# A priority for the layer norms of a chain of four attention blocks

## The chip, the cores and the metric

The kernel runs on one core of one Trainium2 chip. The metric is device time in microseconds (us) of one execution; the profile is of one further execution of the same kernel. Engines are named as in the profile: PE (TensorE matmul), PEld (its weight loads), DVE (VectorE), ACT (ScalarE), POOL (GpSimd) and SP (SyncE, which issues DMAs).

## What is computed

For 64 examples, x is 128 rows of 128 numbers and the context has 77 rows of 128. Four blocks follow one another, and each contains layer norms:

```python
# block 0
norm_X   = ln(context, norm1);  norm_F = ln(x, norm2)
cross    = gelu(attention(norm_F, norm_X, norm_X) @ fc1.T + b) @ fc2.T + b
norm_c   = ln(cross, norm3)
x = norm_F + gamma2 * (cross + gamma1 * attention(norm_c, norm_c, norm_c))
# block 1
x = ln(x + linear_attention(elu(x), elu(context), context), gamma, beta)
# block 2
q = ln(x, sa_ln);                x = x + mha16(q, q)            # 16 heads of 8
x = x + mha16(ln(x, ca_q_ln), ln(context, ca_kv_ln))
x = x + mixture_of_8_experts_top2(ln(x, moe_ln))
# block 3
x1 = ln(x + mha16_causal(x, x), g1)
x2 = ln(x1 + mha16(x1, context), g2)
out = ln(x2 + relu(x2 @ W1 + b1) @ W2 + b2, g3)
```

A layer norm takes each row's mean and variance over 128 numbers, then (row - mean) / sqrt(variance + 1e-5), times a scale, plus a shift.

## The kernel before

**Tiling.** Four examples make a group (NB = 4), so there are 16 groups, and two groups make a set (SG = 2) for the experts. A tile of a group is 128 partitions by 4 x 128 numbers.

**Stages.** `front` is blocks 0 and 1 for a group, `middle` the two attentions of block 2 and the router, `dispatch` and `experts` the mixture for a set, and `second_half` adds the experts' answers and does block 3. Each is a Python generator that yields between steps. The main loop at the end of the program takes one step of each in turn: `firsts` (the middle of group t beside the front of group t+1), `sends` (dispatch), `seconds` (experts), and one or two lanes of `second_half`. So the code records its instructions with the steps of several groups interleaved.

**Order.** A scheduler then gives every engine one list of instructions. Each instruction gets a rank, a counter at the place where the code records it. Where several instructions of an engine are ready at once, the scheduler takes the one of lowest rank. It also finds the tiles their places in memory: a tile name has a fixed number of buffers, and its user waits for one to be free. On the chip every engine works through its own list, with semaphores between the engines.

**The norm.** `normalize` (L269) does the part of a layer norm before scale and shift. For its four examples it has 13 instructions on DVE and one on POOL: four statistics (L274, tile `st`), four means and variances (L276, `mv`), the addition of epsilon (L278, `ve`), the power -0.5 on POOL (L280, `rs`), and four (x - mean) * rs (L283, tile `xh`, or `xm` for the expert norm). `st`, `mv`, `ve` and `rs` have 4 buffers each, `xh` two, `xm` three. It is called 10 times per group, 160 times in all: for C (the context, L470), X (L501), ca (L526), xa (L576, whose scaled result is x1), x1 (L583, for the self-attention of block 2), x2 (L586, cross-attention), x3 (L591, experts) and three times in `second_half` (L830 and L835 after the two attentions, L842 at the end).

**What follows a norm.** Mostly `transposed` (L292): four transposes on PE (L296) into a PSUM tile `bank` (three buffers, used by nearly all PE work), then a scaled copy by ACT (`affine_t`, L303). `affine` (L288) scales and shifts the untransposed result on DVE (L289, L290; in two places L290 is on POOL).

**Other work named below.** In `mha`: the projections (L340, L344), KX (L349 on DVE, L353 on ACT), `vpad` (L364), the bias added to the residual on POOL (L371), then per example the scores (L387, into `banks`), maximum (L396), difference (L398), exp (L399), transposes (L409) and their copies pT (L410), the weighted sum (L417), the copy oT (L425), transposes (L428), division (L431, L432), and at the end the output projection (L456) and the residual add (L460). In `front`: kp (L487, L491), ca (L524), xa (L571). In `middle`: the router and its gates (L595 to L622), their transposes (L627), gT (L629), the product with the experts' bias (L632) and x3b (L634). In `dispatch`: L671 to L733 on DVE, and the indirect DMAs of POOL to the experts' rows (L739). In `experts`: L782, L787, GELU he (L792), L794, the copy ye (L800). In `second_half`: indirect DMAs that fetch answers (L817), their addition to x4 (L821), the feed-forward (L645, L654, L840).

Of the kernel before, what the change touches and what calls it, by code (L numbers as in the profile page):

```python
# [69 lines left out]
def tile_xattn_chain(  # L70
# [197 lines left out]

    def normalize(src, p=P, pool=work, tag="xh", bufs=None):  # L269

        st = small.tile([P, NB, 6], F32, tag="st", name="st")
        mv = small.tile([P, NB, 2], F32, tag="mv", name="mv")
        for b in range(NB):
            V.bn_stats(st[:p, b, :], src[:, b, :])  # L274
        for b in range(NB):
            V.bn_aggr(mv[:p, b, :], st[:p, b, :])  # L276
        ve = small.tile([P, NB], F32, tag="ve", name="ve")
        V.tensor_scalar(ve[:p], mv[:p, :, 1], EPS, None, ALU.add)  # L278
        rs = small.tile([P, NB], F32, tag="rs", name="rs")
        G.tensor_tensor(rs[:p], ve[:p], mhalf[:p], ALU.pow)  # L280
        xh = pool.tile([P, NB, P], F32, tag=tag, name=tag, bufs=bufs)
        for b in range(NB):
            V.tensor_scalar(  # L283
                xh[:p, b, :], src[:, b, :], mv[:p, b, 0:1], rs[:p, b : b + 1], ALU.subtract, ALU.mult
            )
        return xh[:p]
# [180 lines left out]
    def front(st):  # L467
        X, C = st["X"], st["C"]
        Cx = C[:, :, 0:P]
        ch = normalize(Cx, SK)  # L470
        cps = transposed(ch, SK)
        nXT = work.tile([P, NB * SK], F32, tag="nXT", name="nXT", bufs=1)
# [26 lines left out]


        xh = normalize(X)  # L501
        nF = work.tile([P, NB, P], F32, tag="nF", name="nF", bufs=1)
        affine(nF, xh, "n2_w", "n2_b", G)
# [20 lines left out]
        V.tensor_tensor(ca, ps.rearrange("q (b d) -> q b d", b=NB), bc(row["fc2_b"], 1, NB), ALU.add)  # L524
        yield
        xh = normalize(ca)  # L526
        nxT = affine_t(xh, "n3_w", "n3_b")
        nx = work.tile([P, NB, P], F32, tag="nx", name="nx", bufs=1)
# [458 lines left out]
```

## Time and profile before

| | |
|---|---|
| median of 3 runs | 3913.91 us (3906.8 to 3919.5) |
| profiled execution, its own time | 3934.11 us |
| its span, first to last instruction | 3932.3 us |
| mean granted PE clock | 0.832 |
| DVE statistics L274 | 640 instructions of about 0.277 us |
| DVE mean and variance L276 | 640 of about 0.152 us |
| DVE L278 | 160 of about 0.18 us |
| POOL L280 | 160 of 1.027 us |
| DVE L283 | 640 of about 0.34 us at the median |

In the profile, a group's line gives the line of the program, the engine and the operation, then what it writes and reads, the count, the busy time and the mean time of one. The list of waits says which instruction waited for which: total us, times, and the longest. A line of the timeline gives start, duration, engine, line, operation and shapes, and in brackets how long the engine was idle before it and what ended that. Successive short instructions of DVE overlap a little, so four statistics of 0.277 us span some 0.87 us. PE matmul ends are modelled. Names in the trace carry no numbers: x stands for x1, x2, x3 and others.

### The profile page before, as it was taken

Reading aid. Unit: us, or ns where it says so; the run is one execution under the profiler, and the core shown is the slowest. Engines: PE = TensorE matmul, PEld = TensorE weight load, DVE = VectorE, ACT = ScalarE, POOL = GpSimd, SP = SyncE. Lnnn points to the kernel's source line nnn. Section 1 sums busy time; section 2 is a strip of 40 time slices with the busy share of each in tenths; the row PEclk is TensorE's granted clock in tenths of the full one; section 3 lists DMA queues with packets and bytes.
Section 4 is the critical chain, followed back from the end, with each engine's and each line's share of the span. In section 5 each row is a group of like instructions: output and inputs, shape, how many; then the busy total and the mean of one; then the engine's idle time right before and its main releaser. Section 6 shows DMA issues by size and latency. Waiting matters only on the chain. (4 is left out here: it accounts for less than half of the span.)

```text
span 3932.3 us, 59072 instructions
## 1 busy us (share of the span) xinstructions
PE 3022.6 (77%) x22735; PEld 2063.3 (52%) x22797; DVE 2153.0 (55%) x5292; ACT 1977.9 (50%) x2994; POOL 519.4 (13%) x506
## 2 busy tenths in 40 slices
PE   3675677778778778787778877878878888878777
PEld 2454455545455555555455555656545555545544
DVE  5656454456465564555556645566445635445354
ACT  2443353545365554555454635656446556536344
POOL 1002101110211101101211012010210121020110
PEclk9776776878788787978788977989778989989988
DMA  5001111110111111111111011111111132222100
GB/s 178 2 10 35 45 37 55 48 43 30 47 37 43 46 37 33 43 38 52 39 32 53 28 55 39 41 37 36 37 46 40 43 104 65 63 83 64 62 8 6
DMA packets 168257, 180.81 MB, mean 46 GB/s; under 512 B 15708, under 2 KB 111784, under 8 KB 167848
## 3 DMA queue, kind: packets, MB, share of 16 engines
q1 hardware_dynamic: 157936, 157.03, 12.8%
q0 software_dynamic: 8192, 16.79, 1.4%
q8 instruction: 181, 2.97, 0.3%
q10 hardware_dynamic: 1848, 3.19, 0.2%
q14 instruction: 100, 0.82, 0.1%
HBM read 133.54 MB, written 43.42 MB: 45 GB/s over the span
## 5 line engine op out<-in xcount | busy, mean ns | idle before, releaser
L410 ACT COPY pT<-bank 77x512 f32<-77x512 f32 (+1 forms) x1024 | 565.8, 584 | 454.1 <-PE bank L409 410.5
L409 PE MATMUL bank<-ident,pr 128*128 128x128 f32 (+1 forms) x4096 | 661.5, 304 | 146.6 <-ACT pr L399 89.1
L396 DVE TENSOR_REDUCE m<-banks 128x8 f32<-128x1024 f32 (+1 forms) x512 | 514.6, 1005 | 432.3 <-PE banks L387 431.7
L409 PEld LDWEIGHTS bank<-ident,pr 128*128 128x128 f32 (+1 forms) x4096 | 506.7, 158 | 358.8 <-ACT pr L399 134.4
L398 DVE TENSOR_TENSOR pr<-banks,m 128x1024 f32<-128x1024 f32 (+1 forms) x512 | 513.7, 1003 | 26.7 <-PE bank L409 3.1
L399 ACT ACTIVATE pr<-pr 128x1024 f32<-128x1024 f32 (+1 forms) x512 | 451.5, 888 | 122.9 <-DVE pr L398 120.7
L387 PE MATMUL banks<-KX,QT 32*128 32x512 f32 (+1 forms) x2048 | 450.7, 659 | 51.7 <-DVE pr L398 39.6
L280 POOL TENSOR_TENSOR rs<-ve,mhalf 128x4 f32<-128x4 f32 (+1 forms) x160 | 164.4, 1027 | 2379.7 <-DVE ve L278 2379.3
L417 PE MATMUL po<-pT,vpad 77*32 77x128 f32 (+1 forms) x8192 | 435.3, 290 | 17.9 <-issue 8.2
L417 PEld LDWEIGHTS po<-pT,vpad 77*32 77x32 f32 (+1 forms) x8192 | 246.1, 112 | 145.8 <-issue 109.0
L794 PE MATMUL bank<-we,he 128*128 128x128 f32 x1472 | 246.1, 318 | 63.8 <-ACT he L792 60.7
L794 PEld LDWEIGHTS bank<-we,he 128*128 128x128 f32 x1472 | 209.9, 220 | 131.5 <-ACT he L792 103.7
L787 PEld LDWEIGHTS bank<-xT,we 128*128 128x128 f32 x1472 | 229.8, 227 | 60.7 <-ACT xT L769 32.6
L787 PE MATMUL bank<-xT,we 128*128 128x128 f32 x1472 | 241.9, 316 | 18.5 <-ACT xT L769 14.4
L296 PE MATMUL bank<-ident,xh 128*128 128x128 f32 (+1 forms) x448 | 97.0, 340 | 196.5 <-DVE xh L283 179.7
L792 ACT ACTIVATE he<-bank 128x512 f32<-128x512 f32 x184 | 109.9, 597 | 236.0 <-PE bank L787 227.8
L431 DVE RECIPROCAL rs<-bank 128x16 f32<-128x16 f32 x256 | 64.8, 253 | 290.3 <-PE bank L428 286.1
L387 PEld LDWEIGHTS banks<-KX,QT 32*128 32x128 f32 x2048 | 135.9, 213 | 144.2 <-issue 92.4
L739 POOL DMA_INDIRECT sent<-xm,rows_i x128 | 126.0, 984 | 525.7 <-DVE m L396 168.7
L296 PEld LDWEIGHTS bank<-ident,xh 128*128 128x128 f32 (+1 forms) x448 | 64.9, 167 | 223.5 <-issue 161.3
L792 ACT ACT_TABLE_LOAD x124 | 159.1, 1283 | 37.5 <-PE bank L787 35.5
L303 ACT ACTIVATE tT<-bank,col_sb 128x512 f32<-128x512 f32 x80 | 62.3, 778 | 182.6 <-PE bank L296 172.8
(242 smaller groups left out, 4055.3 us busy)
## 6 DMA issues: line engine op xcount, KB each, us to landing
we<-in_moe_w_dram SPq DMA_DIRECT2D x368, 256.0 KB
sent<-zero SPq DMA_DIRECT2D x56, 192.0 KB
xe<-sent SPq DMA_DIRECT2D x56, 192.0 KB
answered<-ye SPq DMA_DIRECT2D x56, 192.0 KB
X<-in_x_dram SPq DMA_DIRECT2D x16, 256.0 KB
later_x<-x3b SPq DMA_DIRECT2D x16, 256.0 KB
x<-later_x SPq DMA_DIRECT2D x16, 256.0 KB
out_dram<-y SPq DMA_DIRECT2D x16, 256.0 KB
```

Of the source, the lines that this page charges most:

```text
L280: G.tensor_tensor(rs[:p], ve[:p], mhalf[:p], ALU.pow)
L296: T.transpose(ps[:, b * p : (b + 1) * p], src[:, b, :], ident[:p, :p])
L387: T.matmul(sc[:, g, : NJ * nk].rearrange("q (j k) -> q j k", j=NJ), lhsT=QT[part, b, :], rhs=KX[part, :, b, :nk], start=not is_causal, sto ...
L396: recent["max"] = V.tensor_reduce(m, scores, AX.X, ALU.max)
L398: V.tensor_tensor(pr, scores, bc(m, 3, nk), ALU.subtract)
L399: S.activation(pr, pr, AF.Exp, scale=DH**-0.5)
L409: T.transpose(pt[:nk, j * P : (j + 1) * P], pr[:, i, j, :], ident)
L410: S.copy(pT[:nk, i].rearrange("k j q -> k (j q)"), pt[:nk])
L417: T.matmul(po[32 * g : 32 * g + 32, half * P : half * P + P], lhsT=vp[:nk, b, 4 * half + g, 32 * k : 32 * k + 32], rhs=pT[:nk, g // 2, g % ...
L787: T.matmul(ps[:, c * P : (c + 1) * P], lhsT=we[:, 0, c, :], rhs=xT[:, a * P : (a + 1) * P], start=False, stop=c == NC - 1,)
L792: S.activation(he.rearrange("p c q -> p (c q)"), ps, AF.Gelu)
L794: T.matmul(eo[:, a * P : (a + 1) * P], lhsT=he[:, c, :], rhs=we[:, 1, c, :], start=c == 0, stop=c == NC - 1)
```

## The change

The body of `normalize` is moved into a function `normalized`, and `normalize` calls it inside a block of the scheduler's that lowers the rank by 400 for the instructions recorded in it. At the block's end the counter goes back to where it was. The instructions, tiles, buffers and engines are the same.

```diff
     def normalize(src, p=P, pool=work, tag="xh", bufs=None):
 
+        with tc.high_priority(offset=400):
+            return normalized(src, p, pool, tag, bufs)
+
+    def normalized(src, p, pool, tag, bufs):
         st = small.tile([P, NB, 6], F32, tag="st", name="st")
         mv = small.tile([P, NB, 2], F32, tag="mv", name="mv")
         for b in range(NB):
```

The lines below the change have numbers 4 higher in the kernel after.

## The prediction

> **What bounds the kernel now.** I read the page's first part, then the list of waits, then the groups by form, then stretches of the timeline on VectorE (DVE) and TensorE (PE).
>
> ```profile
> span 3932.3 us, 59072 instructions
> PE 3022.6 (77%) x22735; PEld 2063.3 (52%) x22797; DVE 2153.0 (55%) x5292; ACT 1977.9 (50%) x2994; POOL 519.4 (13%) x506
> ```
>
> ```profile
> PE bank L296 <- DVE xh L283: 179.7, 44, 11.2
> ...
> DVE xh L283 <- POOL rs L280: 146.8, 125, 7.0
> PEld bank L409 <- ACT pr L399: 134.4, 106, 8.6
> ```
>
> No engine is full. PE is busiest at 77%, so some 900 us of the span it stands idle, and the largest single cause is a layer norm: the transposes of L296 wait 179.7 us, 44 times, for the last instruction of a norm (xh, L283). With the waits for the expert norm's result (called xm, same line) it is 200.1 us, spread over 48 of the 160 norms. DVE in turn idles 146.8 us inside norms, waiting for the one operation they have on POOL (L280).
>
> What a norm costs alone, and what stands in its way, shows on DVE and PE here:
>
> ```profile
> 402.55 0.36 DVE L276 BATCH_NORM_AGGREGATE mv<-st 128x2 f32<-128x6 f32 x4
> 402.82 0.66 DVE L460 TENSOR_TENSOR x<-x,bank 128x512 f32<-128x512 f32 x1
> 403.39 0.17 DVE L278 TENSOR_SCALAR ve<-mv 128x4 f32<-128x4 f32 x1
> 403.51 0.29 DVE L274 BATCH_NORM_STATS2 st<-x 128x6 f32<-128x128 f32 x1
> 404.79 2.06 DVE L283 TENSOR_SCALAR xh<-xa,mv,rs 128x128 f32<-128x128 f32 x4 [0.98 <-POOL rs L280]
> 406.77 0.28 DVE L274 BATCH_NORM_STATS2 st<-x 128x6 f32<-128x128 f32 x1
> 406.97 0.67 DVE L289 TENSOR_TENSOR x<-xh,row_sb 128x512 f32<-128x512 f32 x1
> 407.56 0.28 DVE L274 BATCH_NORM_STATS2 st<-x 128x6 f32<-128x128 f32 x1
> 407.77 0.67 DVE L290 TENSOR_TENSOR x<-x,row_sb 128x512 f32<-128x512 f32 x1
> 408.36 0.28 DVE L274 BATCH_NORM_STATS2 st<-x 128x6 f32<-128x128 f32 x1
> 408.56 0.35 DVE L276 BATCH_NORM_AGGREGATE mv<-st 128x2 f32<-128x6 f32 x4
> 408.84 1.54 DVE L491 SCALAR_TENSOR_TENSOR kp<-kp,kr 77x512 f32<-77x512 f32 x1
> 410.31 0.15 DVE L278 TENSOR_SCALAR ve<-mv 128x4 f32<-128x4 f32 x1
> 411.66 1.11 DVE L283 TENSOR_SCALAR xh<-x,mv,rs 128x128 f32<-128x128 f32 x4 [1.20 <-POOL rs L280]
> ```
>
> ```profile
> 412.15 1.16 PE L296 MATMUL bank<-ident,xh 128*128 128x128 f32 x4 [10.81 <-DVE xh L283]
> ```
>
> The input of the second norm (x2) is complete at 403.5, and its last xh ends at 412.8. Between its four statistics stand L289, L290 and L491 of other streams, which nobody is waiting for, while PE stands idle for 10.81 us. A norm with nothing in between takes 1.35 us for statistics, mean and variance, 1.20 us until POOL has answered, and 1.11 us for the four xh: 3.7 us.
>
> **What the Trainium skill says.** "PSUM — Partial Sum Buffer", section "Engine vs sequencer instructions": the queues of ScalarE, VectorE and GpSimdE are strict FIFO, and matmuls start in program order. The trace agrees: the PE line above has nothing else between 401.3 and 412.2, so the scheduler's order decides, and an instruction that waits holds all behind it. [...]L280 works on four numbers per partition and takes 1.03 us, where DVE's L278, of the same shape, takes 0.17. "Perfetto Trace Analysis", section "Roofline": where matmul and HBM utilization are both low, the kernel is bound by latency. Here PE is at 77% busy, not low, but with 23% waits it agrees in part: what shortens a chain helps only if PE waits on it.
>
> **The change part by part.** Nothing is added or removed; durations stay. Each of the 160 norms issues 13 instructions on DVE and one on POOL, and no DMA. All get a rank 400 places earlier. The instructions executed around a norm lie mostly within some 150 places of its own place in the code's order, so 400 is more than every competitor has: a norm's instruction goes ahead of whatever is ready on its engine, and the true data waits remain.
>
> What it can't move: in the order as executed the first writers of each tile name stand in the order of the code, without exception (2,354 `bank` tiles, 160 `st` tiles). So the norms keep their order among themselves, and PE's users of `bank`, which are nearly all, keep theirs. The inputs C and X are loaded long before, but their norms start only after the norm before them, and this stays. I therefore expect no norm to run far ahead; only local reordering on DVE.
>
> *The gain.* For each of the 48 norms that PE waits for I added the DVE time of foreign instructions between the moment its input was written (and the norm before it had begun) and its last xh, leaving out what fits in the POOL answer. I took the smaller of that and the wait. By kind (norms, wait, removable): ca (L526) 9, 27.9, 20.1 us; x2 (L586) 10, 74.9, 22.2; x1 (L583) 3, 31.6, 0; x3 (L591) 9, 20.3, 2.1; 3s xs (L830) 8, 17.2, 5.9; 3c xs (L835) 9, 28.1, 5.5. Sum 55.8 us of 200.1. The rest is the norms' own 3.7 us, two in a row, or the residual add before. Waiting of L280 behind other work on POOL (indirect DMAs of L739 and L817 among it) adds at most 13 us; I take 0, since POOL is 13% busy and what delays it are waits, not rank. Bounds of the gain: 28 (half is late next for another reason) and 69.
>
> *The loss.* The foreign instructions go behind the norm. For every one that stood inside a norm I took the norm's DVE time still to come, where some engine's wait ended on exactly that instruction (no slack). On PE these are 23.7 us: scores waiting for L398 and others 6.3, x4 and O before L296 4.7, the router chain before L627 and L632 10.3, the start 2.4. On ACT they are 24.2 us (exp after L398 13.2, KX 4.4, gate 5.6 and less), of which half should reach PE: 12.1. Of all foreign time inside norms, 90.6 of 215.5 us belong to the C and X norms of the next group, whose results nobody waits for soon: there the change only costs. On POOL, L280 in front of an L371, L290 or indirect DMA costs these 1.03 us; their own waits are long, so I count 0, at most 10. On SP nothing is moved. Bounds of the loss: 12 (half of PE's part) and 58 (all of both, and POOL's 10).
>
> *Cost at nothing.* DVE will stall the 1.2 us for POOL in nearly all norms instead of 141 of 160: 19 x 1.2 = 23 us of DVE idle, covered since DVE has 45% idle; without cover it is in the bounds of the loss.
>
> *Sum.* 55.8 - 23.7 - 12.1 = 20.0 us. The profiled execution took 3934.1 us (3932.3 span and 1.8 around it), 20 us or 0.5% above the median of the runs, 3913.9. It would become 3914.1; from the median I predict 3894. Next late after a norm is ACT's scaled copy of the transposes (L303), as now.
>
> **The rivals.** *Absorbed:* PE's order is fixed, so PE resumes earlier and then waits as much longer for the next chain (exp L399 ends 89 us of PE waits, pT 42, he 61). For it: 700 us of PE's idle time belongs to other waits. Also here: the rank hardly bites, because few competitors are ready at once. Against: the foreign time inside norms is measured. Some 5 us remain: 3909.
>
> *Slower:* the C and X norms, and x1's, stand at the turn of each group together with the router chain (L597 to L629), on which PE waits at L627 and L632 for 23.8 and 16.0 us already:
>
> ```profile
> 2312.31 1.01 PE L627 MATMUL bank<-ident,gate 128*8 128x128 f32 x4 [6.40 <-DVE sums L678]
> ```
>
> X's statistics (1.35 us) and the rest of C's norm (0.8 + 1.1) would go ahead of that chain: 3.25 us in 16 turns are 52 us at most. With only half the gain, 28, and the whole of the no-slack delays, 23.7 + 24.2 = 48, it ends at +20: 3934. It decides from the point where the delay of these chains exceeds what PE saves at L296; on my numbers a doubled delay or a halved gain, with the ACT half arriving whole.
>
> *More than forecast:* the displaced work has slack after all (no loss): 3914 - 56 = 3858.
>
> **Chances.** Forecast (3870 to 3902) 0.40; more than forecast 0.08; absorbed 0.27; slower 0.25. The resolution is 0.3%, 12 us: faster is under 3902, slower over 3926. That gives faster 0.47, same 0.28, slower 0.25. The range goes from the full gain with little loss (3860) to the slower case (3938).
>
> **What would show it.** Right: L296's wait for xh falls from 200 to about 145 us, and foreign instructions between a norm's statistics and its xh disappear; x2's norm at the place shown takes 3.7 us instead of 9.3. The loss shows as more waiting at L627, L632, L387 and of ACT at L399; absorbed shows as PE idle still near 890 us with the share of L296 smaller. Wrong: if norms of C and X begin far earlier than the norm before them, or `bank` users change order on PE, my view of the fixed order is false, and the time can leave the range either way.

## The result, and the profile after

The kernel after took 3895.74 us (median of 12 runs, 3879.48 to 3905.65) against 3917.45 us for the kernel before beside it (12 runs, 3902.81 to 3924.71): a ratio of 0.9947, 95% interval 0.9931 to 0.9963. In a second session, with 11 and 40 runs, it was 0.9952 (0.9935 to 0.9969). So the change saves some 20 us; 3894 was predicted. The account behind that number does not hold, as the next sections show.

The page of the kernel after begins with these lines:

```profile
span 3893.9 us, 59149 instructions
PE 2985.6 (77%) x22797; PEld 2033.7 (52%) x22797; DVE 2153.9 (55%) x5292; ACT 1982.7 (51%) x2998; POOL 522.4 (13%) x506
```

The waits of the kernel after (instruction, what it waited for, total us, times, longest):

```profile
PEld bank L413 <- ACT pr L403: 151.4, 114, 11.3
PE bank L300 <- DVE xh L287: 131.6, 32, 11.1
...
DVE xh L287 <- POOL rs L284: 111.4, 114, 4.2
```

The wait at the transposes (L296 before, L300 now) fell from 179.7 to 131.6 us. DVE did not stall more on POOL, as predicted, but less: 146.8 us became 111.4.

The norm of x2 that the prediction showed, on DVE in the kernel after:

```profile
395.81 2.06 DVE L287 TENSOR_SCALAR xh<-xa,mv,rs 128x128 f32<-128x128 f32 x4 [0.84 <-POOL rs L284]
397.79 0.28 DVE L278 BATCH_NORM_STATS2 st<-x 128x6 f32<-128x128 f32 x1
398.00 0.36 DVE L280 BATCH_NORM_AGGREGATE mv<-st 128x2 f32<-128x6 f32 x4
398.27 0.65 DVE L293 TENSOR_TENSOR x<-xh,row_sb 128x512 f32<-128x512 f32 x1
398.85 0.16 DVE L282 TENSOR_SCALAR ve<-mv 128x4 f32<-128x4 f32 x1
398.92 0.68 DVE L495 SCALAR_TENSOR_TENSOR kp<-kp,kr 77x512 f32<-77x512 f32 x1
400.51 1.11 DVE L287 TENSOR_SCALAR xh<-x,mv,rs 128x128 f32<-128x128 f32 x4 [0.92 <-POOL rs L284]
```

and on PE:

```profile
401.00 1.15 PE L300 MATMUL bank<-ident,xh 128*128 128x128 f32 x4 [8.99 <-DVE xh L287]
```

The reordering is what was said: the kp of L495 (L491 before) now lies in the time in which POOL answers, and L294 comes after xh. The size is not. From the input's completion (394.19) to the last xh (401.62) the norm takes 7.4 us, against 9.3 before and 3.7 in the prediction, because the norm of xa, which has the priority too and is earlier in the code, still stands in it with its four xh (2.06 us) and its stall, and L293 besides. PE waits 8.99 us here, against 10.81. Over all 160 norms, the DVE time of foreign instructions between the first statistic and `ve` (other norms' instructions not counted) fell from 1.22 to 0.29 us per norm, and between the first and the last xh from 0.39 us to nothing.

**The same pair on one chip.** The first trace of the kernel before was its slowest run, so both kernels were traced again side by side (the experiments e5 and e11). The kernel before again:

```profile
span 3915.1 us, 59134 instructions
PE 3019.6 (77%) x22797; PEld 2060.7 (53%) x22797; DVE 2154.7 (55%) x5292; ACT 1978.4 (51%) x2994; POOL 519.6 (13%) x506
```

and the kernel after again:

```profile
span 3898.9 us, 59149 instructions
PE 2989.5 (77%) x22797; PEld 2034.3 (52%) x22797; DVE 2152.9 (55%) x5292; ACT 1981.0 (51%) x2998; POOL 522.5 (13%) x506
```

One thing is added, although the source adds nothing: ACT runs 2,998 instructions instead of 2,994. The four are ACT_TABLE_LOADs (281 before, 285 after, 1.28 us each) and follow from ACT's new order. They are 5.1 us of ACT's time; whether they lengthen a wait of PE was not separated.

The span fell by 16.2 us, and PE's busy time by 30.1 us. The same 22,797 matmuls ran at a mean granted clock of 0.831 before and 0.838 after; 0.831 / 0.838 x 3019.6 would be 2994. PE's idle time (gaps over 0.1 us, added up from the trace) did not fall: it was 878.9 us before and 893.4 after. That is the main finding. The waits of PE in the kernel before again:

```profile
PE bank L296 <- DVE xh L283: 181.2, 44, 11.2
PE bank L409 <- ACT pr L399: 89.3, 58, 7.8
PE bank L340 <- ACT tT L303: 21.7, 27, 0.9
PE bank L296 <- DVE xm L283: 18.7, 10, 4.3
PE bank L632 <- DVE gT L629: 15.8, 8, 5.9
PE bank L787 <- ACT xT L769: 14.8, 22, 3.9
```

and in the kernel after again, the same six and one that is new among the long ones:

```profile
PE bank L300 <- DVE xh L287: 133.6, 33, 10.9
PE bank L413 <- ACT pr L403: 102.0, 60, 10.5
PE bank L636 <- DVE gT L633: 27.4, 7, 10.4
PE bank L344 <- ACT tT L307: 26.1, 30, 2.5
PE bank L631 <- DVE gate L626: 23.3, 5, 8.7
PE bank L791 <- ACT xT L773: 21.7, 24, 4.9
PE bank L300 <- DVE xm L287: 18.0, 9, 4.3
```

The transposes wait 48.3 us less for a norm (199.9 to 151.6). Against that stand 12.7 us more for exp, 15.1 at the end of the router (all gaps before L627 and L632: 39.3; before L631 and L636: 54.4), 6.9 for xT, 4.4 for tT, and the rest in small pieces: 62.9 us in all, since idle rose by 14.6.

**Where the time went.** Milestones of both traces: the last group's router transposes (L627, L631) began at 3120 and 3124 us, and the rest took 795 and 775 us. So in this pair nothing is gained while groups are turning over, and all of it in the last part, where the second half of the last groups runs alone and no norm of C or X is left. One pair doesn't settle the earlier part: the first two traces have 3138 and 3116 us there, and the two of before differ by 18 us among themselves. The last part repeats. Where the norms of `second_half` keep their place, that last part took 794 to 797 us in four traces (the two of before, e2, e12) and 786 in a fifth (e3); in the nine where they have the priority, it took 774 to 780. The lines give busy time and instructions of PE, PEld, DVE, ACT and POOL, then granted clock, DMA share and GB/s. Kernel before again:

```profile
3120.00:3915.00 795.00, 622.52 (x4982) 421.24 (x4979) 383.14 (x801) 398.32 (x609) 100.37 (x98) 0.89 0.18 56
```

Kernel after again:

```profile
3124.00:3899.00 775.00, 608.71 (x4983) 413.26 (x4981) 381.77 (x802) 397.77 (x609) 101.74 (x98) 0.91 0.19 58
```

Of the 20 us, 14 are PE's busy time at the higher clock and 6 are idle time (160 to 154 us).

**Why the clock differs.** The trace also records the granted clock itself, period by period. It has two values only, 0.5 and 1.0, in periods that are multiples of 3.413 us. The Trainium skill, "TensorE: Matmul & The Clock Gate", Part 1, section "What's actually happening", says that PE's clock is halved after an idle window of about 3.4 us and comes back after a busy one; its section "HAM oscillation — how this bites in real kernels" warns of idle gaps of that length between bursts. The traces of the pair agree on the steps and the two values, but not on the condition: no whole idle window was needed for the fall (e5 has 126 falls and only 50 idle gaps of PE over 3.4 us). I cut the record into stretches of 3.413 us and took PE's busy share of each:

| this stretch, the next | before (e5): count, mean busy share | after (e11) |
|---|---|---|
| full, then full | 607, 0.87 | 621, 0.87 |
| full, then half | 126, 0.42 | 125, 0.41 |
| half, then half | 261, 0.66 | 246, 0.63 |
| half, then full | 126, 0.98 | 125, 0.99 |

A full stretch under 0.4 busy was followed by half clock every time (52 of 52 in each trace), one between 0.5 and 0.6 busy in 22 of 51 before and 21 of 49 after. Every return came after a stretch at least 0.79 busy, but a stretch busy from end to end did not always bring it: 105 of 181 before, 100 of 166 after. The clock is not only a matter of how the trace draws a matmul: successive transposes of L409 start 213 ns apart at half clock and 109 ns apart at full (medians, e5).

The kernel before ran 1324 us at half clock, the kernel after 1266. PE's busy time inside these periods fell by 62.0 us (1012.0 to 950.1), and outside of them rose by 31.9 (2007.5 to 2039.4), which together is the 30.1 us: much the same work, at twice the speed. So in this account the change pays by the shape of PE's waiting, not by its amount. It is an account of two traces and no experiment. No run changed the clock alone, and part of the 14.6 us of idle time may come from the clock, since a PE that is done sooner waits longer for the same chain.

In the last part the shape is plain to see: of PE's idle gaps over 6.8 us there are three, together 24 us, in each of the five traces where the norms of `second_half` keep their place, and one, of 7 to 8 us, in the nine others; in this pair the time at half clock falls there from 170 to 140 us.

### The profile page after: what moved, and what is told of

Same layout as the page of the kernel before. It is cut to its first block, busy times and chain, and to the rows that moved or that the text cites. A ratio compares the mean times of both kernels' runs of the same rounds, so it can differ in the third digit from the quotient of the medians.

```text
span 3893.9 us, 59149 instructions
## 1 busy us (share of the span) xinstructions
PE 2985.6 (77%) x22797; PEld 2033.7 (52%) x22797; DVE 2153.9 (55%) x5292; ACT 1982.7 (51%) x2998; POOL 522.4 (13%) x506
## 5 line engine op out<-in xcount | busy, mean ns | idle before, releaser
L391 PEld LDWEIGHTS banks<-KX,QT 32*128 32x128 f32 x2048 | 133.9, 214 | 149.3 <-issue 88.4
L300 PE MATMUL bank<-ident,xh 128*128 128x128 f32 (+1 forms) x448 | 90.2, 329 | 148.3 <-DVE xh L287 131.6
L796 ACT ACT_TABLE_LOAD x126 | 161.7, 1283 | 39.7 <-PE bank L791 37.6
L821 POOL DMA_INDIRECT ans<-answered,rows_i x128 | 123.8, 967 | 199.9 <-DMA we<-in_moe_w_dram 51.9
L300 PEld LDWEIGHTS bank<-ident,xh 128*128 128x128 f32 (+1 forms) x448 | 62.1, 162 | 168.7 <-issue 131.0
```

Source lines behind the costliest of these rows:

```text
L300: T.transpose(ps[:, b * p : (b + 1) * p], src[:, b, :], ident[:p, :p])
L391: T.matmul(sc[:, g, : NJ * nk].rearrange("q (j k) -> q j k", j=NJ), lhsT=QT[part, b, :], rhs=KX[part, :, b, :nk], start=not is_causal, sto ...
L796: S.activation(he.rearrange("p c q -> p (c q)"), ps, AF.Gelu)
```

## The experiments

Theory at the start: the eight other norms gain some 50 us and the norms of C and X, whose results nobody awaits, give back part. Rivals: C and X cost nothing; any norm put first helps; displaced router work cancels the gain. Ratios are to the kernel before on the same chip, with 95% intervals. In all but e5, e6, e11 and e12, `normalize` got a parameter, called `first` here, that takes the priority from single calls.

**e1, e2: the two sides apart.** e1 leaves the priority to all norms but two; e2 has it for these two only.

```diff
-        with tc.high_priority(offset=400):
+        with tc.high_priority(offset=400) if first else nullcontext():
...
-        ch = normalize(Cx, SK)
+        ch = normalize(Cx, SK, first=False)
...
-        xh = normalize(X)
+        xh = normalize(X, first=False)
```

> Priority for eight of the ten norms of a group; those of the inputs C and X keep their ordinary rank. The theory of the prediction (the gain comes from the norms that PE waits for; C and X only cost, by pushing the router chain and the other lane's softmax back): faster than the changed kernel by about 8 to 14 us, so 30 to 36 us below the kernel before, with the waits at L631 and L636 (54 us in the changed kernel) back near 40. Rival (the C and X norms cost nothing that counts): within 5 us of the changed kernel.

Measured: 3791.09 us against 3841.74, ratio 0.9876 (0.9847 to 0.9905). This is 0.9876 / 0.9947 = 0.993 of the kernel after, 27 us. The two priorities on C and X do cost, twice what was thought.

> Priority for the norms of C and X alone. The theory: 8 to 14 us slower than the kernel before, L631 and L636 waiting about 54 us in place of 40, L300's waits for xh still near 200. Rival (any earlier norm helps, since all norms run in one order and C and X stand before others): 5 to 15 us faster than before.

Measured: 3880.62 us, ratio 1.0103 (1.0074 to 1.0133), so 39 us slower, three times the expected price. The cost did not stand where it was expected: the two gaps at the router's end came to 41.0 us, little more than before, and the waits of the transposes rose instead to 218.5 us (183.2 for xh, 35.3 for xm). C's and X's instructions went into the norms of x1, x2 and x3: between the first statistic and the last xh of these norms, DVE's time on them rose from 10.8 us (e5) to 70.5. Here all eight of their statistics stand in the norm of x3 (tile xm), before its `ve`:

```profile
2281.41 0.87 DVE L278 BATCH_NORM_STATS2 st<-x 128x6 f32<-128x128 f32 x4
2282.20 0.36 DVE L280 BATCH_NORM_AGGREGATE mv<-st 128x2 f32<-128x6 f32 x4
...
2282.65 0.85 DVE L278 BATCH_NORM_STATS2 st<-C 77x6 f32<-77x128 f32 x4
2283.43 0.85 DVE L278 BATCH_NORM_STATS2 st<-X 128x6 f32<-128x128 f32 x4
2284.20 0.15 DVE L282 TENSOR_SCALAR ve<-mv 128x4 f32<-128x4 f32 x1
...
2285.55 1.11 DVE L287 TENSOR_SCALAR xm<-x,mv,rs 128x128 f32<-128x128 f32 x4 [0.81 <-POOL rs L284]
```

In the change itself those norms have the priority too, and this time is 12.2 us in e11, hardly more than before. So e2 prices a harm that the change hardly does; what C and X cost within the change is read from e1. That C and X cost nothing and that any earlier norm helps are both refuted. The two sides do not add up exactly (-49.7 and +38.9 in the means, -10.8 together).

**e3, e4: which of the eight.** e3 keeps the priority for ca and x2, e4 for the three norms of `second_half`.

> Priority for the norms of x2 and ca alone, which had 42 of the 56 us that the prediction called removable. The theory: about 20 us below the kernel before, L300's waits for xh near 160. Rival (the gain comes from the last third of the run, where the profile of the changed kernel won 36 of its 38 us after 2315 us, and few of these norms run): under 8 us below.

Measured: 3810.74 us, ratio 0.9929 (0.9902 to 0.9956). The waits for xh and xm were 157 us, as expected, and two norms of ten gain as much as all ten do.

> Priority for the three norms of the last block alone. The theory: 11 us of removable waits, so 5 to 10 us below the kernel before. Rival (the last third of the run decides): 15 us or more below.

Measured: 3832.27 us, ratio 0.9975 (0.9960 to 0.9990). Small, in the expected range, and its last part took 777 us where 795 is usual.

**e8: how far ahead.** e1 with `offset=40`.

> The priority for all norms but C's and X's, by 40 places where the change has 400. If most of what stands inside a norm was recorded 40 to 150 places before it, the small lead lets it stay: waits of the transposes for xh and xm near 175 us (152 with 400, 200 before), ratio 0.991 to 0.995. If most of it was recorded just before the norm, 40 is as good as 400: waits near 152, ratio 0.986 to 0.989.

Measured: 3813.82 us against 3849.62, ratio 0.9896 (0.9875 to 0.9917), with 176.8 us of waits for xh and xm. The waits agree with the first reading, that much of what stands inside a norm was recorded over 40 places before it. The time lies between the two and decides nothing.

**e7, e10, e13: further variants of e1.** e7 gives the router's chain the priority too; e10 puts C and X 100 places behind their own place; e13 does both.

```diff
+        with tc.high_priority(offset=400) if first else tc.high_priority(offset=-100):    # e10, e13
...
+        hp = ExitStack(); hp.enter_context(tc.high_priority(offset=400))                  # e7, e13: from lg
...
+        hp.close()                                                                        # to gate
...
+        with tc.high_priority(offset=400): V.tensor_copy(gT, ps[:NE])
```

> The priority for all norms but C's and X's, and also for the router's chain on VectorE from the router's scores to the gate and for gT. If displaced router work is what the other norms' priority costs, PE's waits before the two matmuls of the router's end fall from 41 to some 20 us and the time falls by 8 to 15 us against the kernel with the norms alone, ratio 0.984 to 0.986. If PE then waits as much longer for something else, the two waits fall and the time stays within 5 us, ratio 0.986 to 0.989. If the router's 14 instructions in turn displace norms or softmax, ratio above 0.990.

Measured: 3786.65 us, ratio 0.9840 (0.9813 to 0.9867). The time is in the range of the first reading, but its reason is not seen: the two gaps at the router's end were 39.2 us (20.8 and 18.5) against 41.1 in e1, not 20.

> The priority for eight norms of each group, and the norms of C and X 100 places behind their own place. If these two norms at their own place still displace work that PE waits for, the time falls by another 5 to 12 us against the kernel with the eight alone, ratio 0.984 to 0.986. If they find enough free time of VectorE at their own place, nothing moves, 0.986 to 0.989. If their results come too late for the next group's front, transposes wait longer for xh (over 165 us) and the ratio is above 0.990.

Measured: 3795.99 us, ratio 0.9855 (0.9832 to 0.9879), waits for xh and xm 152.0 us. That their results come too late is refuted; whether it gains anything over e1 the intervals don't tell.

> Eight norms and the router's chain with the priority, the norms of C and X 100 places behind their own place. If the two edits add up: ratio 0.980 to 0.984. If they take the same waits away: 0.984 to 0.987.

Measured: 3858.91 us against 3912.93, ratio 0.9862 (0.9838 to 0.9887). The edits do not add up. The intervals of e1, e7, e10 and e13 overlap: all beat both kernels by about the same, and the part that matters is leaving C and X out.

**e6, e12: what holds C and X back.** Both give xh four buffers instead of two, e6 in the kernel after, e12 in the kernel before.

```diff
-        xh = pool.tile([P, NB, P], F32, tag=tag, name=tag, bufs=bufs)
+        xh = pool.tile([P, NB, P], F32, tag=tag, name=tag, bufs=bufs or 4)
```

> The kernel after, with four buffers for the tile xh where it has two. Theory A, that the C and X norms cost because X's xh stands at the head of VectorE's list while it waits for its buffer (DVE xh waits 23.6 us for PE's transposes in the kernel after): that wait falls below 5 us and the time falls by 10 to 20 us against the kernel after, ratio 0.990 to 0.992. Theory B, that they cost because their statistics and xh stand in front of other work, whatever the buffers: the wait falls too, but the time moves by less than 6 us, ratio 0.993 to 0.996.

Measured: 3859.77 us, ratio 1.0033 (1.0020 to 1.0046). Both readings are wrong. DVE's wait for a buffer is gone, as both said, and the kernel is slower by 1.0033 / 0.9947, some 33 us.

> The kernel before with four buffers for xh, no priority. Theory A, that the two buffers hold back the norms of C and X in the changed kernel and four set their lead free: without the priority four buffers do little, ratio 0.997 to 1.003. Theory B, that four buffers cost by themselves: as much slower against two as in the changed kernel, ratio 1.006 to 1.010.

Measured: 3903.84 us, ratio 0.9979 (0.9966 to 0.9992). Four buffers do no harm by themselves, so in e6 it is the lead of the norms that costs. The order of execution shows how: I counted, for each norm, the foreign DVE instructions that stood before its last xh in the kernel before (e5) and stand behind it now.

| norm | after (e11) | e6 | e1 | e12 |
|---|---|---|---|---|
| C | 12.5 | 13.4 | 1.6 | 0 |
| X | 3.8 | 20.5 | 0 | 2.8 |
| ca | 2.8 | 2.6 | 2.7 | 0 |
| x1, x2, x3 | 3.3 | 3.3 | 3.0 | 0 |
| `second_half` | 1.5 | 1.5 | 1.5 | 0 |

C's norm passes the router's chain (L597 to L622 before) in 9 or 10 of 16 turns. X's would pass as much, and is held only because both buffers of xh are in use. In e6 that hold is gone, and PE's waits at the router's end show it:

```profile
PE bank L631 <- DVE gate L626: 37.9, 4, 12.4
```

**e5, e11: the pair again**, unchanged kernels.

> The kernel before once more, for its trace beside the others on one chip. If the lower TensorE clock of its first trace (0.832) was that execution's alone, its clock is here within 0.004 of the kernel after's and its transposes wait near 200 us for xh and xm; PE's idle time is then 20 to 35 us above the kernel after's.

> The kernel after once more, beside the next two on one chip. If the ratio doesn't hang on the chip: 0.993 to 0.996. If the gain belongs to the chip and its clock: outside of that.

Measured: 3914.39 us (ratio 0.9996, 0.9978 to 1.0014) and 3895.03 us (0.9952). The ratio repeats; the chip of the first session is not on record, so that it repeats on another chip isn't shown. The transposes of e5 wait 199.9 us for xh and xm, as expected. But its clock was 0.831 again, so the low clock was not one execution's, and its idle time was 14.6 us below the kernel after's, not 20 to 35 above. The runs without the trace agree: mean clock 0.8347 in 40 runs of before, 0.8347 in the 10 of e5, 0.8395 in the 11 of e11. At equal clocks the two kernels lie 1 to 8 us apart, against 17.6 in the means:

| granted clock | before, us | after, us |
|---|---|---|
| 0.836 | 3909.2, 3912.9, 3914.4 | 3901.8, 3906.2 |
| 0.837 | 3904.7 to 3909.4 (4 runs, two of e5) | 3897.2, 3901.7 |
| 0.838 | 3901.6 to 3904.8 (4 runs) | 3900.7 |
| 0.840 | 3895.9 | 3894.8, 3895.0 |
| 0.841 | 3896.8 | 3892.6 |

Among runs of one kernel, 0.001 of clock goes with 2.4 to 2.9 us. From this slope I estimate what part of each difference of the means goes with the clock. It is an upper estimate of what the clock causes if, from run to run, longer waits lower the clock too; no run separates the two. The last column is the time at half clock in each kernel's one trace (1324 us in both traces of before).

| kernel | mean clock, it and before | difference, us | goes with the clock | the rest | at half clock |
|---|---|---|---|---|---|
| after (e11) | 0.8395, 0.8347 | -17.6 | -13.0 | -4.6 | 1266 |
| e1 without C, X | 0.8502, 0.8448 | -49.7 | -15.5 | -34.2 | 1133 |
| e2 only C, X | 0.8400, 0.8448 | +38.9 | +13.8 | +25.1 | 1262 |
| e3 only x2, ca | 0.8496, 0.8448 | -30.5 | -13.9 | -16.6 | 1112 |
| e4 `second_half` | 0.8460, 0.8448 | -9.8 | -3.6 | -6.2 | 1191 |
| e6 four buffers | 0.8417, 0.8438 | +12.6 | +5.0 | +7.6 | 1232 |
| e7 router too | 0.8505, 0.8438 | -58.8 | -19.1 | -39.7 | 1146 |
| e8 offset 40 | 0.8450, 0.8438 | -35.7 | -2.8 | -32.8 | 1198 |
| e10 C, X later | 0.8524, 0.8438 | -53.2 | -22.9 | -30.3 | 1126 |
| e12 before, four buffers | 0.8410, 0.8347 | -9.5 | -17.4 | +8.0 | 1242 |
| e13 both | 0.8426, 0.8347 | -54.6 | -21.6 | -33.0 | 1204 |

By this estimate the clock carries most of the gain of the change as a whole; for the kernels that leave C and X alone it carries some 30 to 45% of it (8% in e8), and the larger part is PE's waiting. e12, which touches no priority, gains by the clock alone. Chips differ (both traces of before have low clocks), so the last column compares only rows with the same clock of before.

## Why the prediction was right in its time, and where it was wrong

- **Gain, 55.8 us at L296: confirmed.** Measured 50.8 us in the first pair of traces (200.1 to 149.3) and 48.3 on one chip; near 145 us was said.
- **The norm of x2 in 3.7 us: wrong.** It took 7.4. The prediction named L289, L290 and L491 as what stands in it, and passed over the largest piece in its own lines, the stall and the four xh of xa, which no priority moves since xa's norm comes first.
- **DVE stalls 23 us more on POOL: wrong in sign** (139.2 to 111.4 us for xh on one chip). With several norms in a row, the statistics of the next fill the answer of the one before; the lines below show 0.80 us of stall instead of 1.20.
- **Loss, 23.7 + 12.1 = 35.8 us: this step failed.** PE's other waits grew by 62.9 us, above the upper bound of 58. By place: the router's end was put at 10.3 us and cost 15.1; scores (L387, L380) at 6.3, and their wait for L398 grew by 4.0; exp at half of 13.2 and cost 12.7; KX at half of 4.4, and L387's wait for it grew by 6.9. What the sum leaves out altogether is the *absorbed* rival's mechanism: with PE's order nearly fixed (all but 18 of the 12,045 matmuls into `bank` stand at the same place in both traces), PE comes earlier to the next chain and waits there. That PE waits longer for pT, xT and oT, ACT's copies, speaks for it, since no norm stands in ACT's list; no run tests it apart. Its sign, idle near 890 us with a smaller share of L296, is what the traces show.
- **C and X "only cost": right in kind, far too cheap.** Expected 8 to 14 us in e1 and e2; taking the priority from them gains 27 us. The prediction's "only local reordering" holds on the average for eight norms of ten (0 to 3.3 instructions passed) and not for C (12.5). The order of first writers was kept, 160 norms and 2,354 `bank` tiles without an exception, but that a norm stays behind the norm before it is no brake where those before it run ahead as well.
- **The slower rival's router chain is real** (L631 and L636, +15.1 us), at a third of the 52 us that it was given at most, since C passes it in only 9 or 10 turns of 16, and X is held by its buffers. x1's norm passes part of it in 9 turns, but in e1 too, where the gaps are back at 41.1 us; so x1's lead is not what lengthens them.
- **Sum, -20 us: right number, wrong account.** In PE's idle time the change gave +14.6 us, not -20. What went down was PE's busy time, -30.1 us, with 58 us less at half clock. No term of the prediction asked where PE's waits would put PE's clock. What is left at an equal clock is estimated at -4.6 us, which is what the *absorbed* rival allowed (some 5). So the agreement of 3894 with 3895.7 is luck as far as this sum goes.

One turn shows the router's part. DVE in the kernel after (again):

```profile
2301.05 0.28 DVE L278 BATCH_NORM_STATS2 st<-C 77x6 f32<-77x128 f32 x1
2301.25 0.36 DVE L280 BATCH_NORM_AGGREGATE mv<-st 77x2 f32<-77x6 f32 x4
2301.53 0.26 DVE L278 BATCH_NORM_STATS2 st<-X 128x6 f32<-128x128 f32 x1
...
2303.04 1.11 DVE L287 TENSOR_SCALAR xh<-C,mv,rs 77x128 f32<-77x128 f32 x4 [0.80 <-POOL rs L284]
2304.07 0.28 DVE L278 BATCH_NORM_STATS2 st<-X 128x6 f32<-128x128 f32 x1
2304.27 0.36 DVE L280 BATCH_NORM_AGGREGATE mv<-st 128x2 f32<-128x6 f32 x4
2304.55 0.15 DVE L601 TENSOR_TENSOR lg<-bank,router_b_sb 128x32 f32<-128x32 f32 x1
```

PE in the kernel after (again):

```profile
2299.83 0.59 PE L599 MATMUL bank<-router_sb,tT 128*128 128x8 f32 x4
2309.11 1.01 PE L631 MATMUL bank<-ident,gate 128*8 128x128 f32 x4 [8.68 <-DVE gate L626]
```

DVE and PE at the same turn in the kernel before (again):

```profile
2302.83 0.19 DVE L597 TENSOR_TENSOR lg<-bank,router_b_sb 128x32 f32<-128x32 f32 x1 [0.51 <-PE bank L595]
```

```profile
2301.73 1.06 PE L595 MATMUL bank<-router_sb,tT 128*128 128x8 f32 x8 [0.87 <-ACT tT L303]
2309.18 1.01 PE L627 MATMUL bank<-ident,gate 128*8 128x128 f32 x4 [6.39 <-DVE sums L678]
```

Before, the router's scores are taken 0.04 us after the matmul's end (2302.79). After, they have been ready since 2300.42, and C's norm and X's statistics stand in front until 2304.55. The router's matmuls had ended 2.4 us earlier (the view begins at 2300 us and shows four of the eight); the gate's transposes come no earlier (2309.11 and 2309.18), and PE waits 8.68 us instead of 6.39. Here a lead is lost again before one's eyes.

## What to carry to other kernels

Give a priority only to the chains that the bound engine is waiting for: here eight of ten equal norms were worth some 48 us (e1), and the two whose results nobody awaited gave 27 of them back, since a lead of 400 places let these pass whole chains, stopped only by a full buffer. A shorter wait is no gain until the engine's total idle time has fallen: add that up before and after, and put busy time and clock beside it. On PE it matters besides how the waiting is spread, since here a stretch of 3.4 us that was more than 60% empty always halved its clock, and only a stretch that was nearly or wholly full brought it back.

## What the runs showed of the hardware

- The mean granted clock belonged to the order of the instructions, repeatably: on one chip 0.8347 (before, 40 runs, and again 0.8347 in 10), 0.8395 (after, 11) and 0.8410 (e12, 22), with the same matmuls in all. The rule behind it, with the busy shares 0.42 and 0.98 (means), is read from where the record changes in two traces; no run here set such gaps on purpose.
- DVE's priority moved ACT's table loads: 281 in the kernel before, 285 after, 283 in e1, from the same source instructions.
- Chips differed: the kernel before took 3912.9, 3849.6 and 3841.7 us (medians) at mean clocks of 0.8347, 0.8438 and 0.8448.
- Which edit of an order lengthens or shortens the time at half clock could not be told from the sums of waits: e12 has a PE idle time of 894 us against 879 in e5, and still less time at half clock. That stays open.
